# Causal attention units in three pieces of keys, with loads and context work moved

## Chip, cores and metric

One core of a Trainium2 chip runs the whole program. The metric is device time in microseconds; before is the median of three runs.

## The reference, cut to what matters

The program is a decoder of two layers over `x` of shape 4 x 512 x 256 (batch, positions, features) with a context of 4 x 1601 x 256. The change lies in the second layer's causal self-attention and its neighbours:

```python
# 4 batches, 16 heads of 16 features, T = 512
qkv = einsum('btd,ed->bte', x, w_qkv)                 # three 256-wide projections
scores = einsum('bhqd,bhkd->bhqk', q, k) * SCALE
scores = scores + (1 - tril(ones(T, T))) * -10000.0   # causal
out = einsum('bhqk,bhkd->bhqd', softmax(scores), v)
x = layernorm(x + out.reshape(b, t, 256) @ w_out.T)
# then cross-attention of the same x to 1601 context rows (rotary queries and keys, mask),
# then a layernormed feed-forward block
```

Before it come a recurrent layer, a cross-attention and a layer of eight routed experts; the change does not touch them.

## The kernel before

All of the second layer stands in `last_layer`. It is built twice, for `causal` true and false, and a flag computed on the chip chooses; the true form runs here. Its order is written out by hand (`tc.manual_schedule`): each engine executes its instructions in the order in which the code emits them.

**Units.** A unit is (batch b, group g of four heads, cross or not). `units` lists 16 self units (four batches by four groups), then 16 cross units. A group's four heads lie in four strips of 32 partitions, so that four matmuls of 32 rows can share the PE array. `qt[g]` and `kself[g]` hold queries and keys of a group; row 16 of a strip of queries holds the negated maximum of each query, so that the scores come out with the maximum subtracted.

**A self unit, before.** It has four rounds, one for each 128 keys k. A round holds, in two halves of two heads each:

- `scores(u, k, half, h)`: one matmul of keys k against the queries from k*128 on (512, 384, 256, 128 columns), line 1612, into a PSUM bank of its own;
- `next1()`: one slot of the maxima of a later unit, which are computed ahead. A slot takes two heads and one block t of 128 queries against the keys up to that block (128 to 512 columns, line 216, tile `most`), and a reduction with the causal additive mask for each head (line 1573). A self unit has eight slots; the order of t is 2, 3, 0, 1. A cross unit has 26 (line 1571);
- `exponents`: ACT's exponential per head (line 1622) and POOL's `affine_select` per half, which clears the upper triangle of the diagonal block (line 1625);
- `weighted(u, k)`, one round late: four matmuls of 32 columns each (line 1647) into one bank. ACT copies the first into `ot` (line 1657), and DVE adds the other three (line 1660).

When the last slot of a unit is done, `negated` reduces and transposes the maxima and writes them into `qt` by four small DMAs (line 1601, `nrows`). At the start of a self unit, four slots beyond its own are done (`lead`). Units 14 and 15 take one more slot per half round, so that the maxima of unit 16, the first cross unit, are ready.

All PSUM tiles of the layer come from one pool of eight banks, used in turn.

**Work between.** Four lists per unit hold other work. `starts[i]` runs at the start of unit i. `extras[i]` is spread over the rounds. `quiet[i]` gives one item per half round. What is left of either runs at the unit's end. The items that matter here:

- `self_rows(b, c)`: the projections K and Q of batch b for two groups (PE, ACT, then a write to DRAM, since heads change partitions), and `rows`, which loads keys and queries of both groups back (SP, line 1336). They lie in `extras[i+1+2c]` and `starts[i+2+2c]`, with i the first unit of batch b-1.
- `finish(u)`: `divided` (transposes of `ot` and the division); after a batch's last group also `turned`, four `projected` (projection, addition to `x`, moments), and the normalization in `quiet`; then `forward(0)` and `forward(1)` (transposes of the normalized `x`, line 1726) at the head of `extras[index[u] + 2]`.
- `combined(b)`: gathers the expert rows of batch b, adds, normalizes and transposes them.
- `context(b, keys, values)`: keys and values of the context. A key item projects (ACT line 1477), rotates (DVE shuffle and three POOL or DVE operations, lines 1443 to 1446) and writes to `kcd[b]`. A value item is a projection and ACT's copy (line 1491). Its input `cx` is loaded in chunks by ACT's queue (line 1461).
- `cross_queries(b, c)`: rotated queries for the cross units, with loads of their own.

All DMAs of SP's and ACT's queues share eight completion semaphores in turn, so a DMA also waits for the one that had its semaphore before.

**Ahead of unit 0**, the code runs the values of batch 0, some of its keys, the first `self_rows`, the self values, eight value items of batch 1. K and Q of the second pair of groups (`k1_`, `q1_`), the remaining keys of batch 0 and the loads `rows1` are at the head of `extras[0]`.

Of the kernel before, what the change touches and what calls it, by code (L numbers as in the profile page):

```python
# [17 lines left out]
P = 128  # L18
# [23 lines left out]
def decoder(ctx: ExitStack, tc: tile.TileContext, a: dict, out: bass.AP):  # L42
# [1261 lines left out]
    def last_layer(causal):  # L1304

        with ExitStack() as s4:
# [35 lines left out]
            starts = [[] for _ in range(len(units) + 3)]  # L1342
            state = {}
# [67 lines left out]
            def self_rows(b, c, tile=raw_tile):  # L1411
# [9 lines left out]
                def rows():  # L1421
                    for g in (2 * c, 2 * c + 1):
                        from_rows(kself[g], ksd[b], g)
                        from_rows(qt[g], qd[b], g)

                return [lambda: item("qkvK", ksd[b], 1.0), lambda: item("qkvQ", qd[b], QS)], rows
# [82 lines left out]
            def cross_queries(b, c):  # L1509
# [10 lines left out]
                def rows():  # L1520
                    flush(0)
                    for g in (2 * c, 2 * c + 1):
                        from_rows(qt[g], qd[b], g)

                return [item], rows


# [4 lines left out]
            def slots1(u):  # L1532
                return 2 * (1 + NT * NBIG) if u[2] else 2 * NT

            def slot1(u, s):
# [27 lines left out]
                t, c = ((i - 1) // NBIG, (i - 1) % NBIG) if cross else ((i + 2) % NT if causal else i, 0)  # L1563
                n = (t + 1) * P if causal and not cross else 512
                for j, rows, ps in tiles:
                    mm(ps[:, :n], [(qt[g][rows, t * P : (t + 1) * P], kt[rows, c * 512 : c * 512 + n])])

                def reduce():
                    for j, rows, ps in tiles:
                        if cross:  # L1570
                            nc.vector.tensor_reduce(pm[:, t, j, c : c + 1], ps, AX.X, ALU.max)  # L1571
                        else:
                            nc.vector.tensor_tensor_reduce(  # L1573
                                out=ps[:, :n],
                                in0=ps[:, :n],
# [29 lines left out]
            def scores(u, k, half, h):  # L1605
                b, g, cross = u
                kn = kn_of(k) if cross else P
                kt, q2 = keys_of(u), state["q2", u]
                ps = one("s")
                rows = slice((2 * half + h) * 32, (2 * half + h) * 32 + 32)  # L1610
                q0 = seen(u, k)
                nc.tensor.matmul(  # L1612
                    ps[:kn, q0:], kt[rows, k * P : k * P + kn], q2[rows, q0:], start=True, stop=cross or causal
                )
                return ps

            def exponents(u, k, half, pair):
                kn = kn_of(k) if u[2] else P
                ex = p4.tile([P, 2, S], F32, tag="ex", name="ex", bufs=4)
                for h, ps in enumerate(pair):  # L1620
                    q0 = seen(u, k)
                    nc.scalar.activation(ex[:kn, h, q0:], ps[:kn, q0:], AF.Exp)  # L1622
                if causal and not u[2]:
                    block = ex[:, :, k * P : (k + 1) * P]
                    nc.gpsimd.affine_select(  # L1625
                        out=block, in_=block, pattern=[[0, 2], [1, P]], compare_op=ALU.is_ge,
                        fill=0.0, base=0, channel_multiplier=-1,
                    )
                state["ex", u, k, half] = ex
# [8 lines left out]
            def weighted(u, k):  # L1638

                b, g, cross = u  # L1640
                kn = kn_of(k) if cross else P
                po = one("po")
                q0 = seen(u, k)
                for j in range(4):
                    ex = state["ex", u, k, j // 2]
                    c0 = (4 * g + j) * VW
                    nc.tensor.matmul(  # L1647
                        po[j * 32 : j * 32 + 32, q0:],
                        (vals if cross else vself)[b % 2][:kn, k, c0 : c0 + 32],
                        ex[:kn, j % 2, q0:],  # L1650
                        start=True,
                        stop=True,
                    )
# [562 lines left out]
```

## Time and profile before

| | |
|---|---|
| median of three runs | 2037.76 us (2034.16 to 2040.95) |
| the profiled execution | 2031.6 us, span 2029.7 us |
| mean granted TensorE clock | 0.989 |
| busy: PE, DVE, ACT, POOL | 1972.0, 1152.6, 1058.8, 633.7 us |
| self units (first exponent 927.1 us, first of the cross units 1215.7 us) | 288.6 us |
| cross units, first exponents | 1215.7 to 1877.0 us for the last |

How to read it: busy times are shares of one execution, and PE's ends are modelled, so that a busy PE may still wait. Durations in a group are means of one instruction. Rows of the timeline give the start, the length, the engine, the line and the tiles; a bracket gives idle time before the row and what ended it.

### The profile page before, as it was taken

How to read it: one execution, taken by the hardware profiler on the slowest of the kernel's cores; microseconds unless marked ns; L12 is line 12 of the kernel's file. 1: busy time of each engine (PE TensorE's matmuls, PEld its weight loads, DVE VectorE, ACT ScalarE, POOL GpSimd, SP SyncE). 2: the span in 40 equal slices, each digit the busy share in tenths (PEclk: the TensorE clock that was granted, in tenths of full speed). 3: DMA queues.
4: the chain of work that ended last, by engine and by line, in shares of the span. 5: the costliest groups of instructions: out<-in, count | busy, mean ns of one | idle time of the engine just before them, and what ended most of it. 6: DMA issues, size and time to landing. Idle time of an engine off the chain costs nothing.

```text
span 2029.7 us, 33782 instructions
## 1 busy us (share of the span) xinstructions
PE 1972.0 (97%) x12736; PEld 1223.4 (60%) x12736; DVE 1152.6 (57%) x2871; ACT 1058.8 (52%) x2220; POOL 633.7 (31%) x657
## 2 busy tenths in 40 slices
PE   9999999999999999988899999999999999999998
PEld 5768677787899999964455553333333433333366
DVE  3455334442233333356666697677778788887333
ACT  1111222124554555634556537787778788878631
POOL 3010001131222222234632324555655365353110
PEclk9999999999999999999999999999999999999999
DMA  9930411116887786743422111111210120102000
GB/s 365 352 105 1 165 65 54 54 68 257 308 311 292 256 323 265 291 124 109 137 59 59 51 53 42 43 47 58 76 45 28 35 87 18 33 18 85 1 11 33
DMA packets 80109, 242.61 MB, mean 120 GB/s; under 512 B 14134, under 2 KB 37084, under 8 KB 68028
## 3 DMA queue, kind: packets, MB, share of 16 engines
q1 hardware_dynamic: 59948, 141.45, 20.4%
q0 software_dynamic: 13152, 85.64, 11.1%
q10 hardware_dynamic: 6832, 13.20, 2.0%
q8 instruction: 105, 1.72, 0.3%
q14 instruction: 72, 0.59, 0.1%
HBM read 194.47 MB, written 56.69 MB: 124 GB/s over the span
## 4 chain that ended last, share of the span: by engine, by line
PE 48%; DVE 4%; ACT 1%; POOL 1%; issue 1%; DMA 1%; SPq 0%; ACTq 0%; POOLq 0%; DVEq 0%
PE one L216 12%; PE s L1612 12%; PE po L1647 11%; PE most L216 10%; DVE pm L1571 2%; DVE most L1573 1%; PE one L1678 1%; POOL x L188 1%; ACT ex L1622 1%; ACT x L178 0%; PE one L1703 0%; DVE st L163 0%; DMA kcd<-raw 0%; POOL ot L1664 0%; DVE ot L1660 0%
## 5 line engine op out<-in xcount | busy, mean ns | idle before, releaser
L1622 ACT ACTIVATE ex<-s 128x512 f32<-128x512 f32 (+4 forms) x1088 | 526.1, 565 | 177.6 <-PE most L216 97.4
L1571 DVE TENSOR_REDUCE pm<-most 128x1 f32<-128x512 f32 x768 | 477.7, 682 | 93.2 <-PE most L216 91.8
L216 PE MATMUL most<-kc,qt 32*128 32x512 f32 (+1 forms) x2048 | 425.2, 535 | 0.7 <-ACT ex L1622 0.4
L1612 PE MATMUL s<-qt,kc 32*128 32x512 f32 (+1 forms) x1664 | 409.0, 618 | 1.3 <-DMA qt<-nrows 1.3
L1664 POOL TENSOR_TENSOR ot<-ot,part 128x512 f32<-128x512 f32 x180 | 228.1, 1268 | 278.6 <-ACT part L1663 278.2
L1612 PEld LDWEIGHTS s<-qt,kc 32*128 32x128 f32 (+1 forms) x1664 | 133.8, 180 | 171.0 <-ACT ex L1622 125.4
L1647 PE MATMUL po<-ex,v 128*32 128x512 f32 (+1 forms) x1664 | 225.1, 605 | 0.0
L216 PEld LDWEIGHTS most<-kc,qt 32*128 32x128 f32 x2048 | 171.4, 185 | 53.3 <-issue 19.3
L1102 DVE TENSOR_TENSOR g<-g,sg 128x1024 f32<-128x1024 f32 (+1 forms) x38 | 45.5, 1197 | 215.3 <-ACT sg L1100 215.3
L1573 DVE CUSTOM_DVE_ANT_0 most<-most,c_diagq 128x384 f32<-128x384 f32 (+3 forms) x256 | 118.4, 519 | 39.0 <-PE most L216 28.2
L216 PE MATMUL wide<-xbT,eWg 128*128 128x128 f32 (+1 forms) x928 | 135.3, 306 | 1.9 <-ACT g L1100 1.9
L216 PE MATMUL wide<-xbT,eWi 128*128 128x128 f32 (+1 forms) x928 | 134.6, 305 | 0.0
L216 PEld LDWEIGHTS wide<-xbT,eWg 128*128 128x128 f32 x928 | 126.3, 194 | 8.7 <-ACT g L1100 2.1
L216 PE MATMUL bank<-eWo,g 128*128 128x256 f32 x592 | 130.8, 379 | 0.0
L216 PEld LDWEIGHTS wide<-xbT,eWi 128*128 128x128 f32 x928 | 125.6, 192 | 8.2 <-issue 0.8
L1647 PEld LDWEIGHTS po<-ex,v 128*32 128x32 f32 (+1 forms) x1664 | 34.5, 108 | 150.1 <-ACT ex L1622 145.3
L216 PEld LDWEIGHTS bank<-eWo,g 128*128 128x128 f32 x592 | 111.1, 190 | 14.3
L1663 ACT COPY part<-po 128x512 f32<-128x512 f32 x180 | 106.7, 593 | 7.3 <-PE po L1647 6.4
L1625 POOL TENSOR_SCALAR_AFFINE_SELECT ex<-ex 128x256 f32<-128x256 f32 x128 | 52.5, 417 | 157.2 <-ACT ex L1622 157.2
L1612 PE MATMUL s<-qt,ks 32*128 32x128 f32 (+3 forms) x512 | 97.6, 483 | 3.4 <-DVE at L1682 2.4
L709 POOL DMA_INDIRECT xs<-x,rows x32 | 31.3, 978 | 214.8 <-DVE ltot L695 153.4
L216 PE MATMUL most<-ks,qt 32*128 32x256 f32 (+3 forms) x512 | 92.6, 486 | 5.5 <-ACT v L1491 2.9
(336 smaller groups left out, 2913.9 us busy)
## 6 DMA issues: line engine op xcount, KB each, us to landing
xs<-zero SPq DMA_DIRECT2D x32, 512.0 KB
kc<-kcd SPq DMA_DIRECT2D x16, 800.5 KB
eWo<-in_eWo SPq DMA_DIRECT2D x8, 1408.0 KB
eWi<-in_eWi SPq DMA_DIRECT2D x8, 1028.0 KB
eWg<-in_eWg SPq DMA_DIRECT2D x8, 1028.0 KB
qt<-qd SPq DMA_DIRECT2D x32, 256.0 KB
ctxT<-in_ctxT SPq DMA_DIRECT2D x4, 1601.0 KB
kcd<-in_c_rowkc SPq DMA_DIRECT2D x4, 1601.0 KB
```

Source lines behind the costliest of these rows:

```text
L188: nc.gpsimd.tensor_scalar(into(t), xb[:, t, :], mid["mv"][:, t, 0:1], mid["rs"][:, t : t + 1], ALU.subtract, ALU.mult)
L216: nc.tensor.matmul(ps, l, r, start=(i == 0), stop=(i == n - 1))
L709: nc.gpsimd.indirect_dma_start(xs, bass.IndirectOffsetOnAxis(ap=rows[:, k * NT + t : k * NT + t + 1], axis=0), x[b][:, t, :], None)
L1102: nc.vector.tensor_tensor(part, part, dst, ALU.mult)
L1571: nc.vector.tensor_reduce(pm[:, t, j, c : c + 1], ps, AX.X, ALU.max)
L1573: nc.vector.tensor_tensor_reduce(out=ps[:, :n], in0=ps[:, :n], in1=diagq[:, 384 - t * P : 384 - t * P + n], scale=1.0, scalar=LOWEST, op0= ...
L1612: nc.tensor.matmul(ps[:kn, q0:], kt[rows, k * P : k * P + kn], q2[rows, q0:], start=True, stop=cross or causal)
L1622: nc.scalar.activation(ex[:kn, h, q0:], ps[:kn, q0:], AF.Exp)
L1625: nc.gpsimd.affine_select(out=block, in_=block, pattern=[[0, 2], [1, P]], compare_op=ALU.is_ge, fill=0.0, base=0, channel_multiplier=-1,)
L1647: nc.tensor.matmul(po[j * 32 : j * 32 + 32, q0:], (vals if cross else vself)[b % 2][:kn, k, c0 : c0 + 32], ex[:kn, j % 2, q0:], start=True ...
L1663: nc.scalar.copy(part, po)
L1664: nc.gpsimd.tensor_tensor(state["ot"], state["ot"], part, ALU.add)
```

## The change

A causal self unit has three pieces instead of four rounds: keys 0, keys 2, and keys 1 and 3 together. In the joint piece the scores of a head are two matmuls into one bank (keys 1 in columns 128 to 511, keys 3 in columns 0 to 127), with one exponential of 512 columns, one select over two diagonal blocks, and weighted sums that accumulate both keys in one bank. The maxima have three groups, t = 2 and 0 in one bank, 1, and 3; a unit has six slots, and units 14 and 15 take two more per half.

The loads of keys and queries are split by group: the first group's is issued at the end of the unit that makes them, the second's at the start of the next. For batch 0's cross queries, the first group's load moves one unit forward. `forward` moves one unit back. The gathers of batches 2 and 3 are split six and five between two units instead of eight and three. Ahead of unit 0 come the remaining keys of batch 0, `k1_`, `q1_` and the loads `rows1`, with two value items instead of eight; the other values and some keys of batch 1 move to the extras of units 0 to 3.

```diff
+            def pieces(u):
+                if causal and not u[2]:
+                    return [(0,), (2,), (1, 3)]
+                return [(k,) for k in range(NKT if u[2] else NT)]
+            groups = [(2, 0), (1,), (3,)] if causal else [(t,) for t in range(NT)]
+            def spans(u, ks):
+                if len(ks) == 1:
+                    return [(ks[0], seen(u, ks[0]), seen(u, ks[0]), S)]
+                return [(k, seen(u, k), 0 if i else seen(u, k), S - seen(u, k) if i else S) for i, k in enumerate(ks)]
...
-                return 2 * (1 + NT * NBIG) if u[2] else 2 * NT
+                return 2 * (1 + NT * NBIG) if u[2] else 2 * len(groups)
...
+                for t, cols, n in wide_:
+                    for j, rows, ps in tiles:
+                        mm(ps[:, cols], [(qt[g][rows, t * P : (t + 1) * P], kt[rows, :n])])
...
-                nc.tensor.matmul(
-                    ps[:kn, q0:], kt[rows, k * P : k * P + kn], q2[rows, q0:], start=True, stop=cross or causal
-                )
+                for k, q0, c0, c1 in spans(u, ks):
+                    kn = kn_of(k) if cross else P
+                    nc.tensor.matmul(
+                        ps[:kn, c0:c1], kt[rows, k * P : k * P + kn], q2[rows, q0:], start=True, stop=cross or causal
+                    )
...
+                for i, (k, q0, e0, e1) in enumerate(parts):
+                    kn = kn_of(k) if cross else P
+                    for j in range(4):
...
+                            start=i == 0,
+                            stop=i == len(parts) - 1,
...
-                    extras[index[u] + 2].insert(0, lambda: forward(0))
-                    extras[index[u] + 2].insert(1, lambda: forward(1))
+                    extras[index[u] + 3].insert(0, lambda: forward(0))
+                    extras[index[u] + 3].insert(1, lambda: forward(1))
...
-                    quiet[i - 2] += summed[:8]
-                    quiet[i - 1] += summed[8:]
+                    quiet[i - 2] += summed[:6]
+                    quiet[i - 1] += summed[6:]
...
-                    starts[i + 2 + 2 * c].append(rows)
+                    soon[i + 1 + 2 * c].append(rows[0])
+                    starts[i + 2 + 2 * c].append(rows[1])
...
-                    starts[i + 2 + 2 * c].append(rows)
+                    starts[i + (2 if b else 1) + 2 * c].append(rows[0])
+                    starts[i + 2 + 2 * c].append(rows[1])
...
-            for f in turns0 + self_values(0) + add1 + values1[:8]:
+            for f in turns0 + self_values(0) + keys0[2:4] + keys0[6:8] + [k1_, q1_]:
+                f()
+            flush(0)
+            for f in add1 + values1[:2] + rows1:
                 f()
...
-            extras[0] = [
-                k1_, q1_, *keys0[2:4], lambda: (keys0[6](), keys0[7]()), lambda: (flush(0), rows1()),
-                *values1[8:11],
-            ] + extras[0]
-            extras[1] = values1[11:] + keys1[:2] + extras[1]
-            for i, n in enumerate((2, 5)):
-                extras[i + 2] = keys1[n : n + 3] + extras[i + 2]
+            extras[0] = values1[2:9] + extras[0]
+            extras[1] = extras[1] + values1[9:] + keys1[:2]
+            extras[2] = keys1[2:5] + extras[2]
+            extras[3] = extras[3] + keys1[5:8]
+            for work, loads in zip(extras, soon):
+                work += loads
...
-                        shorter = half and causal and not u[2] and k > 1
+                        shorter = causal and not u[2] and ks == ((2,) if half else (1, 3))
...
-                        if i in (14, 15) and done["n"] < ends1[units[16]] + LEADX:
-                            reduces[half].append(next1())
+                        for _ in range(2 if causal else 1):
+                            if i in (14, 15) and done["n"] < ends1[units[16]] + LEADX:
+                                reduces[half].append(next1())
```

## The prediction

> **What bounds it now.** I read the page first, then windows cut at the first exponent of each self unit (unit 0 to 15), then groups by shape inside 926 to 1215 us, then the timeline.
>
> ```profile
> PE 1972.0 (97%) x12736; PEld 1223.4 (60%) x12736; DVE 1152.6 (57%) x2871; ACT 1058.8 (52%) x2220; POOL 633.7 (31%) x657
> ```
>
> PE is never idle for long anywhere, so 97% says little. The change touches 900 to 1216 us only: the cross units keep their instructions (the moved `forward` of the last batch is the one exception). So the question is what the 290 us of self units lose.
>
> ```profile
> core 0: us, PE busy (x) PEld busy (x) DVE busy (x) ACT busy (x) POOL busy (x), PEclk, DMA share, GB/s
> 926.00:944.43 18.43, 15.34 (x106) 8.40 (x106) 11.34 (x51) 9.69 (x27) 6.98 (x16) 0.91 0.58 184
> ...
> 966.03:990.80 24.77, 21.59 (x134) 11.24 (x128) 15.88 (x49) 10.16 (x24) 21.34 (x24) 0.93 0.54 168
> ...
> 1007.86:1027.51 19.65, 16.55 (x133) 9.74 (x127) 15.44 (x69) 12.06 (x32) 3.25 (x8) 1.00 0.25 69
> 1027.51:1043.22 15.71, 15.57 (x121) 8.64 (x121) 8.83 (x31) 9.65 (x24) 5.51 (x9) 0.89 0.08 18
> ...
> 1169.99:1215.70 45.71, 44.05 (x335) 23.59 (x336) 43.03 (x97) 14.19 (x36) 10.13 (x19) 0.96 0.16 50
> ```
>
> Second column the length, then busy time by engine. Most units are bound by no engine's sum: unit 4 (1007.86) has DVE 15.4 and PE 16.6 in 19.65, and unit 5 runs at a granted clock of 0.89. Only units 14 and 15, which also take unit 16's maxima, are DVE's (43.03 of 45.71). Unit 11 cut into its four rounds shows why a unit without accidents is long:
>
> ```profile
> 1121.72:1125.80 4.08, 4.08 (x36) 2.07 (x32) 1.50 (x9) 2.66 (x5) 0.81 (x2) 1.00 0.00 0
> ...
> 1132.63:1135.50 2.87, 2.85 (x28) 1.41 (x23) 2.87 (x9) 0.89 (x5) 0.81 (x2) 1.00 0.54 161
> ```
>
> The first round (scores 512 wide, maxima 128) is PE's, with DVE 1.5 of 4.08; the last (scores 128, maxima 512) is DVE's, 2.87 of 2.87. Eight banks do not carry work across rounds, so a unit pays the larger engine round by round.
>
> ```profile
> 1018.44 3.72 PE L216 MATMUL one<-outP,atT 128*128 128x256 f32 x16
> ...
> 1024.76 0.30 ACT L132 ACTIVATE sd<-mv,eps 128x4 f32<-128x4 f32 x1 [5.69 <-DVE mv L168]
> ...
> 1027.51 2.02 ACT L1622 ACTIVATE ex<-s 128x512 f32<-128x512 f32 x4
> 1027.65 0.98 PE L1726 MATMUL one<-ident,x 128*128 128x128 f32 x5 [0.16 <-ACT x L178]
> ```
>
> The end of unit 4 (8 and 12 alike): the projection ends at 1022.1, DVE is still at four 512-wide maxima (1018.3 to 1021.0) and reaches the moments late; ACT stands 5.69 us, and the next unit's exponents start 5.4 us after the projection. PE stands on `forward`'s transposes meanwhile, and the clock falls in the next unit.
>
> **The change, part by part.** Rounds are A (piece 0, 512 wide), B (piece 2, 256), C (1 and 3, 384+128).
>
> ```profile
> L1622 ACT ACTIVATE ex<-s 128x512 f32<-128x512 f32 x64 | 33.4, 596 | 23.2 <-PE s L1612 21.6 <-PE most L216 1.4
> ...
> L1622 ACT ACTIVATE ex<-s 128x384 f32<-128x384 f32 x64 | 27.0, 493 | 10.4 <-PE s L1612 10.3
> ...
> L1622 ACT ACTIVATE ex<-s 128x128 f32<-128x128 f32 x64 | 14.3, 275 | 26.8 <-PE s L1612 26.2 <-POOL ex L1625 0.5
> ```
>
> *Instructions removed.* 64 exponents of 384 and of 128 become 64 of 512: 64 x (493+275-596) ns = 11.0 us of ACT. One 128-wide addition a unit goes: 16 x 0.267 us (the shortest row of L1660) = 4.3 us of DVE. Selects go from eight to six a unit, two of them over 512 elements; the trace has only 256 (417 ns), so those cost 417 to 834 and POOL saves 0 to 13 us. Columns on PE and maxima on DVE stay. ACT and POOL end last nowhere in the self units, so this alone is worth 0, save DVE's 0.5 us in units 14 and 15.
>
> *One round fewer.* DVE's maxima per round become 4x512, 4x(384+128), 4x256, beside scores of 512, 256 and 512 columns: the wide maxima no longer meet the narrowest scores. In unit 11, PE's own work is four bursts of scores and maxima at 1.35 (the burst from 1117.55 to 1118.9) = 5.4, weighted sums 0.99+0.78+0.59+0.39 = 2.75 (chain of waits), two projections of 1.91 and transposes of 0.59: 12.6 of 13.78. At most 1.2 us goes; I take 0.8 for units 7 and 11: **1.6**.
>
> *Units 4, 8, 12.* The projection now meets 256-wide maxima: 4 x about 0.38 instead of 4 x 0.65 on DVE, and they precede it, so the moments follow the projection by 1.3 us, not 2.6. I take 1.3 + 0.4 for the round = 1.7 each: **5.1**. ACT's wait stays, since the applies still precede the exponents.
>
> *`forward` one unit later.* Units 5 and 9 lose 0.98 us of transposes; at clock 0.89 over 15.71 they lost 1.7 us, which may stay if the gap stays. I take 2.4 each for round, transposes and part of the clock (bounds 1.0 to 3.5) and 1.5 for unit 13 (at 0.75 now): **6.3**. Units 6 and 10 take the 1.0 over.
>
> *Requests at the end of the unit.* In the changed program's instruction order SP issues these loads in the same sequence as before (rows of nrows, K and Q writes, loads); what changes is the distance to the user. For batch 1, and the second halves of batches 2 and 3, K and Q now stand in an early round: no wait. For the first half of batches 2 and 3, Q is made in unit 5's and 9's last round and used by the maxima of round B of units 6 and 10.
>
> ```profile
> 1107.02 0.61 SPq L1333 DMA_DIRECT2D qd<-raw  x1
> ...
> 1111.57 0.33 SPq L1336 DMA_DIRECT2D qt<-qd  x1
> ```
>
> Write to load issue takes 4.5 us, and the maxima using it start at 1114.43, 8.0 us after Q's evacuation began (1106.39). The new distance is round A, `forward` and two weighted sums, about 5.5: a wait of 2.5. With the transposes taken over I charge 1.0 in unit 6 (which waits 2 already) and 2.2 in unit 10 (bounds 0 to 4 each): **-3.2**.
>
> *More keys, fewer values ahead.* The same PE work in another order. Now the key writes of two chunks pass SP inside unit 0, and ACT's load of `cx` stands behind one of them: ACT idles 4.25 us until 933.44, and PE drops to 0.91. In the new order POOL turns those keys from about 907 and SP has them out by 919, before the maxima of unit 0 end; `nrows` of unit 0 stands behind them and four loads. Those loads wait for the K and Q writes until about 922, DVE's maxima end near 923, so the first scores come 0.8 us later than 926.0 (0 to 4 if POOL is late). Unit 0 then needs about 11.5 us plus its lead against 18.43: 5.0 net. Two values slip into unit 1 (-0.9). Unit 2 loses part of its clock loss (24.77 x 0.07 = 1.7) and a round of waiting behind POOL: 3.3 (0 to 5); unit 3, 1.5. Sum **8.9**.
>
> *Units 14 and 15.* DVE's floor is 43.0-0.5 = 42.5; three slots a half round instead of two use up the slots that ran alone before unit 16: 1.7 of the 3.2 possible. **1.7**.
>
> Sum: 1.6+5.1+6.3-3.2+8.9+1.7 = 20.4, taken as 20. The profiled execution took 2031.6 us (span 2029.7), 6.2 below the median of 2037.76; against itself the change gives 2011.6, against the median **2018**.
>
> **A rule that speaks against it.** In C each head's 384 columns are followed by its own 128, and only then by the next head's 384. Both stand on one row group, so the second head must overtake waiting passes.
>
> ```profile
> 1121.48 0.37 PE L216 MATMUL most<-ks,qt 32*128 32x128 f32 x1
> 1121.59 0.59 PE L1612 MATMUL s<-qt,ks 32*128 32x512 f32 x1
> 1121.70 0.54 PE L216 MATMUL most<-ks,qt 32*128 32x128 f32 x3
> 1122.01 0.59 PE L1612 MATMUL s<-qt,ks 32*128 32x512 f32 x1
> ```
>
> Here both heads' scores stand before both maxima in the program, yet three passes of maxima start ahead of the last pass of scores. So matmuls of other row groups do overtake, one or two waiting ones at least; I take no cost. The Trainium skill (TensorE: Matmul & The Clock Gate, Part 3: Packing small matmuls) states the opposite: matmuls start in program order and only weight loads are pulled ahead. By that rule the sum would be rival 1's 2052 instead of 2018.
>
> **Rivals.**
> 1. *Slower: the joint scores run one head after another.* If three waiting passes cannot be overtaken, C loses its pairs. Passes on one row group follow at 0.54 us for 512 columns and 0.21 for 128 (1120.50 to 1121.04, 1120.83 to 1121.04), so about 0.43 for 384; a head takes 2 x (0.43+0.21) = 1.28, two in turn 2 x 1.28 - 0.21 = 2.35, so 1.07 more, twice a unit, 16 units: 34 us, and 2018+34 = 2052. It decides from about 0.6 us a half. Chance 0.12; another 0.05 for lesser losses (Q's wait at 4 us and a late start).
> 2. *Little gain.* A fills all eight banks and is followed by 2.6 us of maxima; bubbles join rather than vanish, and ACT's 5.69 us stays. Then only unit 0's 5.0 and some 2 elsewhere remain, minus 3.2: 2034. Chance 0.25, 0.16 of it faster, 0.09 the same.
> 3. *The earlier request does nothing*, since SP's order is the same; its part of the forecast is already negative, so this rival lies inside the forecast.
> 4. *More:* no half clock left and units at PE's own work: 15 us beyond, 2003. Chance 0.08.
>
> **How the numbers follow.** Forecast 0.50 (2011 to 2026). What can be told from no change is 0.3%, 6 us. Faster 0.50+0.08+0.16 = 0.74, the same 0.09, slower 0.17. The range goes from rival 4's 2003 to 2042, the milder losses; only rival 1 lies outside.
>
> **What would show it.** Exponents of 512 in round C; unit 4 near 17.9 us and unit 11 near 13; the gap of ACT before `sd` under 5 us; units 6 and 10 longer, with PE waiting for `qt<-qd`; no ACT idle before 940 due to `cx`; the second head's 384 starting within 0.2 us of the first's. It is wrong if that distance is about a microsecond, or if units 5 to 13 keep their lengths.

## The result, and the profile after

The changed kernel takes 2052.34 us in the median of five runs (2047.41 to 2055.32) against 2037.76. Compared over all runs and not by the two medians alone, it takes 1.0061 times as long, 95% interval 1.005 to 1.0072. It is slower, where a gain of 20 us was forecast. The profiled execution took 2052.93 us (span 2051.2, mean granted clock 0.980 instead of 0.989).

The page's first part: ACT lost 7 us of work (11.0 were forecast) and POOL 4, DVE gained 7, and PE counts 6 us more for the same 12736 matmuls.

```profile
PE 1978.2 (96%) x12736; PEld 1230.0 (60%) x12736; DVE 1159.6 (57%) x2855; ACT 1051.9 (51%) x2156; POOL 629.6 (31%) x625
```

Windows cut at the first exponents, with the columns of before: units 1, 4, 8, 9, 10 and 11, and then 14 with 15.

```profile
950.85:980.48 29.63, 25.98 (x145) 14.06 (x147) 10.78 (x42) 11.38 (x25) 6.20 (x10) 0.83 0.28 90
1021.65:1047.96 26.31, 20.88 (x140) 12.37 (x140) 18.27 (x75) 11.81 (x27) 5.79 (x14) 0.87 0.18 51
1093.20:1116.35 23.15, 20.03 (x141) 12.04 (x138) 16.98 (x68) 11.72 (x28) 3.35 (x7) 0.93 0.11 37
1116.35:1128.66 12.31, 11.61 (x105) 6.64 (x108) 7.86 (x32) 8.05 (x18) 2.91 (x6) 1.00 0.10 24
1128.66:1148.36 19.70, 16.91 (x128) 10.65 (x124) 9.90 (x38) 8.39 (x20) 5.19 (x7) 0.83 0.24 69
1148.36:1160.23 11.87, 11.87 (x110) 6.21 (x103) 9.82 (x38) 7.22 (x16) 2.27 (x5) 1.00 0.22 55
1189.74:1234.60 44.86, 44.60 (x331) 24.92 (x327) 42.45 (x85) 14.66 (x30) 11.95 (x17) 0.96 0.17 55
```

Units 9 and 11 run at full clock and, unit 11, at PE's own 11.87 us: there the change did what it promised. Units 4 and 8 (19.65 us in unit 4 before) and 10 are far longer, at clocks of 0.83 to 0.93 and with PE idle for 2.8 to 5.4 us.

The whole sum, in us, by the first exponent of each unit; `before_again` is a second profile of the kernel before (span 2034.9), taken with the experiments:

| part | forecast | after, less the first profile of before | less its second |
|---|---|---|---|
| up to the first `x<-x,nb,rstd` (a normalization on ACT) ahead of unit 0 | 0 | +4.4 | +1.6 |
| from there to the first exponent, units 0 to 3 | -8.9 | +6.2 +3.2 | +5.2 +1.8 |
| units 4, 8, 12 | -5.1 | +9.0 | +8.9 |
| units 5, 9, 13 | -6.3 | -10.9 | -10.9 |
| units 6, 10 | +3.2 | +10.4 | +10.6 |
| units 7, 11 | -1.6 | -2.6 | -2.6 |
| units 14, 15 | -1.7 | -0.9 | -0.9 |
| from unit 16 on | 0 | +2.6 | +2.6 |
| sum (of the unrounded parts) | -20.4 | +21.5 | +16.3 |

From 500 us on the trace of after has 75.3 us at half clock, those of before 37.9 and 48.5. Half of the difference, 13 to 19 us, is what PE can lose by that (an estimate from these lengths); the loss is 16 to 21.

The three units of the row 4, 8 and 12 differ: unit 4 grew by 6.7 us, unit 8 by 3.3, and unit 12 fell by 1.0.

**Units 4, 8, 12.** The timeline at the end of unit 8 (start, length, engine, line, tiles; in brackets idle time and what ended it):

```profile
1106.24 1.09 ACT L1738 COPY atT<-one 128x512 f32<-128x512 f32 x2
1106.89 5.46 PE L216 MATMUL one<-outP,atT 128*128 128x256 f32 x16 [1.70 <-ACT atT L1738]
1108.48 0.42 DVE L1744 TENSOR_TENSOR x<-one,x 128x256 f32<-128x256 f32 x1 [2.73 <-PE one L216]
1113.60 0.30 ACT L132 ACTIVATE sd<-mv,eps 128x4 f32<-128x4 f32 x1 [6.27 <-DVE mv L168]
1116.35 2.02 ACT L1648 ACTIVATE ex<-s 128x512 f32<-128x512 f32 x4
```

The projection `outP` stands behind the last round with nothing beside it. PE waits 1.70 us for the last transposed copy, then runs the sixteen passes in 5.46 us instead of 3.72, since 3.4 us of them are at half clock, and DVE waits for their results instead of being late with its maxima. ACT's gap before `sd` is 6.27 (5.69 before). Unit 4 has the same end, and before it one more wait, for queries, as in units 6 and 10 below:

```profile
1028.22 1.34 PE L216 MATMUL most<-ks,qt 32*128 32x384 f32 x16 [2.41 <-DMA qt<-qd]
```

In unit 12 the projection stands behind the last round too, but PE neither waits nor loses its clock there (3.78 us, ACT's gap 4.58), and the unit takes 19.95 us instead of 20.91. There the place of the projection by itself costs nothing that shows.

**Units 6, 10.** The timeline at the start of unit 10:

```profile
1127.61 0.61 SPq L1333 DMA_DIRECT2D qd<-raw  x1
1132.19 0.33 SPq L1336 DMA_DIRECT2D qt<-qd  x1
1134.89 2.11 PE L216 MATMUL most<-ks,qt 32*128 32x384 f32 x16 [2.79 <-DMA qt<-qd]
1136.73 1.09 PE L1638 MATMUL s<-qt,ks 32*128 32x256 f32 x4
1137.88 0.66 ACT L1648 ACTIVATE ex<-s 128x256 f32<-128x256 f32 x2 [5.03 <-PE s L1638]
```

Write to load takes 4.58 us (4.55 before), and the maxima want the queries 2.79 us before they are there. That is the wait that was forecast (2.5). Behind it PE runs at half clock (1134.9 to 1141.7; four score passes of 256 columns end 1.09 us after the first starts, 0.70 at full clock), and this unit's scores stand behind the waiting maxima, so ACT loses 5.03.

**Unit 1** waits for a load that held PE for 1.25 us at most before (in the second profile):

```profile
968.83 0.38 ACTq L1462 DMA_DIRECT2D cx<-in_ctxT  x1
970.23 0.38 ACT L1492 COPY v<-one 65x256 f32<-65x256 f32 x1
973.39 5.37 PE L216 MATMUL one<-cx,xaK 128*128 128x512 f32 x8 [3.65 <-DMA cx<-in_ctxT]
```

The values end the use of one `cx` and the keys at once ask for the next, which ACT's queue requests only behind ACT's exponents. Here, too, a step of half clock falls on the eight passes behind the gap: they take 5.37 us, 3.70 in unit 1 of `cx_apart` below, at full clock.

### The profile page after: what moved, and what is told of

It reads as the page before. It is cut to its first block, busy times and chain, and to the rows that moved or that the text cites. A ratio compares the mean times of both kernels' runs of the same rounds, so it can differ in the third digit from the quotient of the medians.

```text
span 2051.2 us, 33601 instructions
## 1 busy us (share of the span) xinstructions
PE 1978.2 (96%) x12736; PEld 1230.0 (60%) x12736; DVE 1159.6 (57%) x2855; ACT 1051.9 (51%) x2156; POOL 629.6 (31%) x625
## 4 chain that ended last, share of the span: by engine, by line
PE 48%; DVE 3%; POOL 2%; ACT 2%; DMA 2%; issue 1%; another core or an unknown queue 0%; SPq 0%; ACTq 0%; POOLq 0%; DVEq 0%
PE s L1638 12%; PE one L216 12%; PE po L1678 11%; PE most L216 10%; DVE pm L1584 1%; PE one L1710 1%; ACT x L178 1%; POOL x L188 1%; DMA qt<-qd 1%; ACT ex L1648 0%; DVE most L1599 0%; DMA qd<-raw 0%; POOL raw L1447 0%; POOL swp L1446 0%; POOL raw L1445 0%
## 5 line engine op out<-in xcount | busy, mean ns | idle before, releaser
L1648 ACT ACTIVATE ex<-s 128x512 f32<-128x512 f32 (+2 forms) x1024 | 519.2, 589 | 166.9 <-PE most L216 106.6
L1655 POOL TENSOR_SCALAR_AFFINE_SELECT ex<-ex 128x256 f32<-128x256 f32 (+1 forms) x96 | 46.5, 487 | 184.3 <-ACT ex L1648 184.1
L216 PE MATMUL most<-ks,qt 32*128 32x512 f32 (+3 forms) x512 | 85.5, 488 | 11.3 <-DMA qt<-qd 8.3
```

Of the source, the lines that this page charges most:

```text
L216: nc.tensor.matmul(ps, l, r, start=(i == 0), stop=(i == n - 1))
L1648: nc.scalar.activation(ex[:kn, h, c0:], ps[:kn, c0:], AF.Exp)
L1655: nc.gpsimd.affine_select(out=block, in_=block, pattern=pattern, compare_op=ALU.is_ge, fill=0.0, base=0, channel_multiplier=-1,)
```

## The experiments

Ratios are to the kernel before, run alongside on the same chip. Four chips were used, and the median of the kernel before is 2033.4 and 2034.1 us on two of them (chips 1 and 3), 2038.9 to 2039.3 on the others (5 and 6); so ratios can be compared between experiments, times cannot. A is the round of keys 0, B of keys 2, C of keys 1 and 3.

### Is the slow stretch ahead of unit 0 the change's?

`again` is the changed kernel unaltered, `before_again` the kernel before.

> The changed kernel once more, unaltered, for a second profile. In the first profile the products ahead of the first self unit stood still from 877 to 892 us (ACT's copies of v waited 14 us in all) and the first exponent came at 937.7 us, 41.5 us after the first x<-x,nb,rstd. If that standstill is chance, it is absent here, the first exponent comes at about 928 to 932, still 41.5 us (within 1) after x<-x,nb,rstd, and the time is about 2043 to 2048. If it belongs to the changed program it recurs, and the time is about 2052. In both cases units 4, 6, 8 and 10 are as long as in the first profile (26.3, 19.8, 23.1, 19.7 us, each within 1.5).

> The kernel before, unaltered, for a second profile. In its first profile the stretch from the first product of v to the first x<-x,nb,rstd took 18.0 us and began at 873.9 us; in all five profiles of the changed kernel and its variants so far it began at 865.8 to 868.5 and took 27.6 to 27.8 us, with PE standing still in the products of v. If the standstill belongs to the changed program, it is absent here, and the time is about 2032 to 2038. If the first profile of before was the exception, the stretch begins at about 866 and takes 27 us here too, the first exponent comes near 929, and the time is about 2035 to 2040.

2050.57 and 2036.78 us. From the first product of `v` to `x<-x,nb,rstd` the first profile of before had 18.0 us; its second has 26.1, the two of after 27.8 and 27.6. In the later profiles the stretch takes 17.7 to 19.2 or 25.9 to 27.8 us, and it goes with the chip: all eight profiles on chips 1 and 3 have the short length, all nine on chips 5 and 6 the long one, `before_again` among them (for the first profiles of before and after the chip is not recorded). So this is not the change's, and the second profile is the fairer comparison. Why the chips differ stays open. Units 4, 6, 8 and 10 of `again` are as long as in the first profile of after (25.5, 19.3, 23.3 and 19.5 us).

### Which part costs?

`old_ahead`: the order of the work ahead of unit 0, `extras[0]` to `extras[3]` and the split of the gathers as before.

```diff
-quiet[i - 2] += summed[:6]
-quiet[i - 1] += summed[6:]
+quiet[i - 2] += summed[:8]
+quiet[i - 1] += summed[8:]
...
-for f in turns0 + self_values(0) + keys0[2:4] + keys0[6:8] + [k1_, q1_]:
-    f()
-flush(0)
-for f in add1 + values1[:2] + rows1:
+for f in turns0 + self_values(0) + add1 + values1[:8]:
     f()
...
```

> The changed kernel with the order of work ahead of unit 0 and the keys and values in units 0 to 3 as before the change. Theory: the new order is a loss, since four more rotations of keys stand ahead of the sums of x and of unit 0's maxima: the first exponent comes 35 to 36 us after the first x<-x,nb,rstd instead of 41.5, units 0 to 3 take about 81 us in all instead of 84, and the time falls by 9 us to about 2043. Rival: the order is neutral, unit 0 grows by what the start gains (unit 0 was 17.3 us before and is 13.1 now), and the time stays at 2049 to 2053. Units 4 to 15 are as in the changed kernel in both.

1.0035 (1.0022 to 1.0048), median 2045.5: the new order costs some 5 us as it stands. From `x` to the first exponent is again 36.2, but units 0 to 3 take 91.2 instead of the 81 expected. The waits of units 0 and 1 say why:

```profile
PE most L216 <- DMA qt<-qd: 12.5, 1, 12.5
```

With three rounds unit 2's maxima begin in the second of unit 0's three rounds (the third of four before), before the queries made at the head of `extras[0]` are loaded. So with three pieces either order costs: the old one 12.5 us of waiting in unit 0, the new one the later start and unit 1's wait. The old one is the cheaper, by some 5 us.

`three_alone`: the kernel before with three pieces and nothing else (the old order as above, `forward` and all requests as before).

> The kernel before with three pieces and three groups of maxima alone; forward, requests and the order ahead of unit 0 as before. Theory: three rounds alone cost 8 to 16 us: units 0 to 3 take about 91 us in all instead of 80.7, units 4, 8 and 12 are 2 to 6 us longer each, units 5, 9 and 13 about 2 shorter; the time is 2046 to 2054. Rival: the pieces alone gain their round (2 to 6 us) and the time is 2032 to 2037.

1.0083 (1.0065 to 1.0101): 17 us slower than before, the most of all (8 to 16 were expected). Unit 0 has the same wait (10.6 us), and units 6 and 10 take 35.2 (29.1 before). `four` undoes only the pieces and the maxima's groups; the order of maxima and scores in a round and the slots of units 14 and 15 go back with them:

```diff
-return [(0,), (2,), (1, 3)]
+return [(0,), (1,), (2,), (3,)]
...
-groups = [(2, 0), (1,), (3,)] if causal else [(t,) for t in range(NT)]
+groups = [(2,), (3,), (0,), (1,)] if causal else [(t,) for t in range(NT)]
...
```

> The changed kernel with four pieces and four groups of maxima as before, and all else as changed (forward a unit later, requests at the end of the unit, more keys ahead). Theory: it is the cut to three rounds that costs, since what was spread over four rounds falls behind the last one or meets its own load: units 4, 8 and 12 come back to 18 to 20 us each, units 5, 9 and 13 stay below before's (13 to 14.5), unit 1 falls from 27 to 29 us to about 20, and the time is 2030 to 2036, below before. Rival: the other three parts cost as much as the pieces; the time is 2042 or more.

1.007 (1.0055 to 1.0086), no better, where a time below before's was expected. Units 4, 8 and 12 fall from 69.4 to 60.1, which shows that the three rounds, with their three groups of maxima, are what costs there; units 5, 9 and 13 rise from 34.2 to 42.8. The two nearly cancel. `four_old` is `four` with the old order ahead as well, so that only the later `forward` and the earlier requests remain of the change:

> Four pieces and the order ahead of unit 0 and in units 0 to 3 as before the change; forward a unit later and the requests at the end of the unit as changed. Theory: with four rounds these two parts gain at most their transposes in units 5, 9 and 13 (2 to 3 us in all) and lose 2 to 7 us in units 6 and 10: the time is 2037 to 2044, so the 13 us that the run with four pieces lost came mostly from the order ahead of unit 0. Rival: they lose as much as the order ahead, 2044 or more; or they gain 6 us and more, 2033 or less.

1.005 (1.0033 to 1.0066). This was the rival's side: with four rounds the two remaining parts cost some 10 us, in units 0 to 3 (86.6) and 6 (22.05). In unit 6 of `four`, which has the later `forward` too, POOL's bias addition lies on DVE's weighted additions of the gathers:

```profile
1062.05 2.37 POOL L1763 TENSOR_TENSOR x<-x,bob 128x1024 f32<-128x1024 f32 x1
1062.35 3.60 DVE L1386 SCALAR_TENSOR_TENSOR x<-y,ws,x 128x256 f32<-128x256 f32 x2
...
1067.03 0.70 PE L1638 MATMUL s<-qt,ks 32*128 32x256 f32 x4 [2.98 <-DVE at L1714]
```

The first of the two additions takes 3.06 us there; without an instruction on POOL one takes 0.48. DVE reaches its other work later, and PE waits 2.98 us for DVE's division (3.13 in `four_old`).

`forward_back` and `requests_back` each undo one of these in the changed kernel:

```diff
# forward_back
-extras[index[u] + 3].insert(0, lambda: forward(0))
+extras[index[u] + 2].insert(0, lambda: forward(0))
...
# requests_back
-soon[i + 1 + 2 * c].append(rows[0])
-starts[i + 2 + 2 * c].append(rows[1])
+starts[i + 2 + 2 * c] += rows
...
-starts[i + (2 if b else 1) + 2 * c].append(rows[0])
+starts[i + 2 + 2 * c].append(rows[0])
```

> The changed kernel with forward where it was, two units after the last of its batch. Theory: inside three rounds the later forward is a gain, as it was forecast (6.3 us, less 2 us that units 6 and 10 take over): units 5, 9 and 13 grow from 12.3, 12.3 and 9.6 to about 14.3, 14.3 and 10.4 us, units 6 and 10 fall by about 1, and the time rises by 3 to 6 us to 1.0075 to 1.009 of before's. Rival: the part costs, as with four pieces, because x<-x,bob on POOL now meets the sums of x on DVE in unit 6: the time falls by 3 us or more, to 1.0045 or less.

> The changed kernel with all requests for queries and keys at the start of the next unit. On SP the self units' sequence stays the same; on PE the division of units 5 and 9 moves back to the third round, and nothing else of the self units moves. Theory: the request by itself does nothing: units 4 to 13 keep their lengths within 1 us, the time stays within 3 us of the changed kernel's (1.0046 to 1.0076 of before's). Rival: as items of the list the requests shift the work beside them, and without them the time falls by 4 us or more.

1.0037 (1.0024 to 1.0049) and 1.0053 (1.0035 to 1.0071). `forward` at its old place is 0.24% better than the change, and 0.16% better than `requests_back`, which ran on the same chip; the second difference lies within the two intervals. Units 5, 9 and 13 pay 2.6 us together, but units 6 and 10 take 32.0 instead of 39.5. There the transposes are gone, and the wait for the queries, though it stays (2.10 and 1.93 us), leaves one step of half clock in unit 6 instead of two, and none in unit 10:

```profile
1127.84 1.17 PE L216 MATMUL most<-ks,qt 32*128 32x384 f32 x16 [1.93 <-DMA qt<-qd]
```

The same sixteen passes took 2.11 us behind 2.79 of waiting. The earlier requests make no difference that can be told.

### The three waits, taken away one by one

`weighted_first`: in units 4, 8 and 12 the items of round A run behind its weighted sums, so that `finish`'s pauses fall one round earlier.

```diff
+early = i in (4, 8, 12) and k == 0
-if k and u[2]:
+if k and u[2] or early:
     weighted(*due)
...
-if due and not (k and u[2]):
+if due and not (k and u[2] or early):
     weighted(*due)
```

> The changed kernel, with the last weighted sum of units 3, 7 and 11 issued ahead of the items of the first round of units 4, 8 and 12, so that division, transposes and projection of a batch take one round each of the three. Theory: in the changed kernel the two pauses need four rounds, so the projection falls behind the last round and runs alone (1106.2 to 1112.3 us in unit 8, at half clock, while DVE and ACT mostly wait). Units 4, 8 and 12 fall from 26.3, 23.1 and 20.0 us to 18 to 20 each, 10 to 14 us in all, and the time to about 2040. Rival: ACT's wait for the moments and the clock set these units, not the place of the projection: they fall by under 1.5 us each and the time to no less than 2047.

1.0015 (1.0003 to 1.0026), 2041.52: by the ratio 9.4 us off the change, as expected. Unit 4:

```profile
1018.76:1041.32 22.56, 19.25 (x140) 11.99 (x140) 18.32 (x75) 11.82 (x27) 5.76 (x14) 0.92 0.19 61
...
1033.28 3.72 PE L216 MATMUL one<-outP,atT 128*128 128x256 f32 x16
...
1038.57 0.30 ACT L132 ACTIVATE sd<-mv,eps 128x4 f32<-128x4 f32 x1 [2.55 <-DVE mv L168]
```

The projection lies beside round C at full clock, and ACT's gap falls from 6 us to 2.55. The three units take 63.4 us (22.6, 21.4 and 19.5) instead of 69.4: 6.0 less, where 10 to 14 were expected; units 6 and 10 fall as well, by 3.4 together. In unit 4 the wait for the queries is gone too, and PE waits 2.22 us for DVE instead, so this run does not separate the projection's place from the waits.

`q_early`: Q's projection of units 5 and 9 directly behind K's, in round B, so that its write has a round more.

```diff
-into.insert(min(1, len(into)), divided)
+into.insert(min(2 if index[u] in (4, 8) else 1, len(into)), divided)
```

> The changed kernel, with Q of units 5 and 9 right behind K in the second round and the division in the third. SP's order is unchanged. Theory: the write of Q leaves about 4.5 us earlier, so PE's wait for qt<-qd in units 6 and 10 (2.8 us each) is gone, and with it the half clock of 6.8 us that follows each: units 6 and 10 fall from 19.8 and 19.7 us to 13.5 to 15.5, and the time by 9 to 12 us to about 2041. Rival: the wait and the half clock have separate causes: only the 2.8 us go, units 6 and 10 come to about 17 and the time to about 2047.

1.0001 (0.9991 to 1.0012), 2039.51: by the ratio 12 us off the change. Unit 10:

```profile
1125.51:1139.41 13.90, 13.90 (x131) 8.84 (x127) 10.07 (x38) 8.42 (x19) 5.31 (x8) 1.00 0.22 75
```

19.70 us become 13.90: no idle PE, full clock. The wait itself was 2.79. Unit 6, for which the same was expected, only falls from 19.8 to 18.5: its wait for the queries and its half clock are gone as well, but PE now waits up to 1.5 us at a time for DVE and its own issue. So the two units give 7 of the 12 us in this profile, and where the rest lies is not shown.

`lead2` reaches the same from the other side: the maxima lead the scores by two half groups instead of four.

```diff
-return LEADX if u[2] else 4
+return LEADX if u[2] else 2
```

> The changed kernel with two half groups of maxima computed ahead of a self unit instead of four. Theory: four half groups were two of four rounds and are two of three now, so the maxima of the unit after next ask for its queries and keys a third of a unit earlier than before; with two the wait for qt<-qd in units 4, 6, 8 and 10 is gone (2.4 to 2.9 us each) and the half clock behind it: units 6 and 10 fall from 19.5 to 14 to 16 us, and the time by 6 to 12 us to 2040 to 2046. Rival: the row of maxima (nrows) now reaches its unit's scores too late, and each of 15 units waits 0.5 to 2 us for qt<-nrows: the time stays at 2048 or rises to 2070.

1.0021 (1.0007 to 1.0034), 2039.13; PE waits for no `qt<-qd` in the self units any more, and unit 10 takes 13.5 us. Unit 6 takes 18.7, more than the 14 to 16 expected: the gathers' additions lie beside POOL's bias addition there, as in `four` (the first takes 3.56 us, and PE waits 2.65 for DVE). Units 4, 8 and 12 take 63.0 us (23.3, 20.0 and 19.6), as little as with `weighted_first`, though the projection stays behind round C. A lead of four half groups was two of four rounds and is two of three now: the same number asks for the queries earlier. Units 5, 9 and 13 pay 2.6 us for the shorter lead.

`fix2` is `weighted_first` with `q_early`.

> The changed kernel with both repairs, the weighted sum first in units 4, 8 and 12, and Q right behind K in units 5 and 9. If the two losses are separate they add: each took 9 to 12 us off the changed kernel's time, so 2027 to 2033, below before. If they share their half clocks (units 6 and 10 were already shorter with the first repair alone), the sum is 2033 to 2039.

0.9988 (0.9975 to 1.0001): the two add in part, to the time before (the second of the two cases).

`cx_apart` puts unit 1's own work between the last value and the first key:

```diff
-extras[0] = values1[2:9] + extras[0]
-extras[1] = extras[1] + values1[9:] + keys1[:2]
+extras[0] = values1[2:11] + extras[0]
+extras[1] = values1[11:] + extras[1] + keys1[:2]
```

> The changed kernel with two more values in unit 0 and the last two first in unit 1, so that the first key of batch 1 comes a round or more after the item that asks for its cx. Theory: the wait for cx (4.4 us) and the half clock behind it (two of three windows of 3.4 us there) go: unit 1 falls from 27.3 to 19 to 21 us, unit 0 grows by 1 to 3, and the time falls by 4 to 6 us to 1.003 to 1.0045 of before's. Rival: POOL, busy for 25 of unit 2's 27 us with the turns of the keys, takes it over: unit 2 grows by what unit 1 loses, and the time stays at 1.0052 or more.

1.0012 (1.0 to 1.0024), 2035.72: by the ratio 10 us off the change, more than expected. Unit 1 falls from 29.6 us (27.3 in `again`) to 19.2 at full clock; unit 0, which takes over two value items, grows by 0.5 to 13.7. The wait itself was 3.65. Unit 1's window:

```profile
944.86:964.05 19.19, 19.19 (x139) 10.52 (x140) 11.23 (x42) 10.55 (x23) 5.31 (x9) 1.00 0.37 109
```

### The later start

`sums_first` runs the sums `add1` ahead of the remaining keys, as before:

```diff
-for f in turns0 + self_values(0) + keys0[2:4] + keys0[6:8] + [k1_, q1_]:
+for f in turns0 + self_values(0) + add1 + keys0[2:4] + keys0[6:8] + [k1_, q1_]:
```

> The changed kernel with one group moved on DVE: the eight sums of x of batch 1 (x<-ex,ws,x) stand ahead of the shuffles of the four keys that POOL turns, as before the change, not behind them. In the changed kernel they run from 918.8 to 924.3 us beside POOL's rotations (5.5 us for eight, of 3.8 without) and unit 0's maxima wait behind them on DVE, while PE had the first of them at 919.4. Theory: this order is the loss of the start; the first exponent comes 36 to 38 us after the first x<-x,nb,rstd instead of 41.4, units 0 to 3 keep their 84 to 85 us, and the time falls 3 to 5 us to about 2047. Rival: the maxima wait for the queries and keys or for PE anyway: the start moves by under 1.5 us, the time stays at 2050 to 2053.

1.0049 (1.0033 to 1.0066). From `x` to the first exponent 40.2 instead of 41.4, not the 36 hoped for. SP's queue took the place of the sums: unit 0's last maxima end at 923.94 already, but its `nrows` stand on SP behind the four loads of `rows1`, which wait for the K and Q writes.

```profile
923.21 0.73 DVE L1599 CUSTOM_DVE_ANT_0 most<-most,c_diagq 128x512 f32<-128x512 f32 x1
...
925.18 0.42 SPq L1336 DMA_DIRECT2D qt<-qd  x1
...
925.73 2.31 SPq L1627 DMA_DIRECT2D qt<-nrows  x4
...
930.75 1.22 PE L1638 MATMUL s<-qt,ks 32*128 32x512 f32 x2 [3.29 <-DMA qt<-nrows]
```

`fix3` adds `sums_first` to `fix2`:

> The changed kernel with three repairs: the weighted sum first in units 4, 8 and 12, Q right behind K in units 5 and 9, the sums of x ahead of the shuffles. If the start's loss adds to the others: 2031 to 2035, below before. If the start is hidden behind other waits in units 0 to 3: 2035 to 2038.

0.9991 (0.9975 to 1.0008), no different from `fix2`. The start's 5 us stay with this order.

### A version that beats both

`best` is the change with `lead2`, `weighted_first`, `sums_first` and `cx_apart`; `best_forward_back` has `forward` at its old place besides.

> The changed kernel with four repairs: two half groups of maxima ahead instead of four, the weighted sum first in units 4, 8 and 12, the sums of x ahead of the shuffles, the first key of batch 1 apart from its cx. If the losses add: 0.991 to 0.995 of before's time. If the half clocks come back at other places: 0.996 to 1.000.

> The kernel with the four repairs, and forward back at two units after the last of its batch. If the later forward costs by itself, as in the changed kernel (its time fell by 0.24% without it), the ratio falls from 0.9974 to 0.995 to 0.996. If it cost only through the wait for qt<-qd and the half clock in units 6 and 10, which the repairs have taken away, it is a gain here, as forecast: units 5, 9 and 13 grow by 0.9 each, the ratio is 0.998 to 0.9995.

`best`: 2027.6 us, 0.9974 of the kernel before (0.9957 to 0.9991; 2034.1 us on that chip); the change is at 1.0061, so these four edits are worth about 0.9%. That is the case in which half clocks come back elsewhere. PE waits for no `cx` and no `qt<-qd` in its self units any more. `best_forward_back`: 1.0 (0.9989 to 1.0011), on another chip. With the four repairs the later `forward` is thus ahead by 0.26%, though undoing it in the change as given brought 0.24%. The intervals of each pair all but touch, so the turn is likely and not certain. By the units the gain is not where it was forecast: without the later `forward` units 5, 9 and 13 take 3.3 us more and units 6 and 10 3.4 less (in unit 6 the gathers' additions no longer meet POOL's bias addition, and the unit takes 14.2 instead of 16.7), and the rest of the difference is half clock, in units 4, 8 and 15 and behind unit 16 above all (85.0 us of it from 500 us on against 39.7).

## Why the prediction was wrong

Two terms of the sum that were booked as gains came out as losses, the start with units 0 to 3 and units 4, 8 and 12, and a third, units 6 and 10, was priced far too low. Against the second profile of before they are 16, 14 and 7 us off. The last two, and the wait in unit 4, come from one wrong step: the prediction did not follow the distances that are written as a number of rounds or slots (a pause in a chain, the lead of the maxima) through a unit of three rounds; and it priced a wait of PE at its length, without the half clock behind it.

- **Units 4, 8, 12: the failed step.** The prediction had the projection beside the 256-wide maxima and took 1.7 off each unit. No maxima lie beside it at all. `finish` runs at the end of A, its division and first pause end in B, its transposes and second pause in C, and the projection falls behind C; four rounds had room for two pauses and the projection, three have not. In unit 8 PE then waits 1.70 us for the transposed copy and meets the half clock. In unit 4 it also waits 2.41 us for queries, though the prediction says "no wait" for batch 1. +9.0 instead of -5.1, in units 4 and 8 alone (+6.7, +3.3, and -1.0 in unit 12). That three rounds cost this is shown by `four`, which takes all of it back. How it divides is not: `weighted_first`, which moves the projection, takes 6.0 back, and `lead2`, which leaves it and moves the maxima, 6.4.
- **Units 6, 10: the right wait, the wrong price.** A wait of 2.5 us was forecast and 2.79 came in unit 10, but the charges of 1.0 and 2.2 became 4.4 and 6.1. What was left out is what the wait does to the clock and to the scores queued behind the waiting maxima. The bound of "0 to 4 each" was too tight: without the wait, unit 10 is 5.8 us shorter.
- **Start and units 0 to 3.** Unit 0 gained 4.2 us on the first profile of before and 5.7 on the second (13.1 us), where 5.0 was forecast. The start came 5 to 6 later, not 0.8. Counted from the first `x<-x,nb,rstd`, the forecast had unit 0's maxima done after 31 us and the loads `rows1` after 30. It put POOL's keys and SP's loads in the sum but not DVE's `add1` sums, which moved behind the keys (they start after 22.5 us instead of 12.1) and of which eight take 5.48 us instead of 3.75 beside POOL's rotations: the maxima end after 36. And SP's loads were put too early: the last is issued after 33. In `sums_first` the maxima are done after 31, as forecast, but the loads still end after 32.5, and only 1.2 us come back; so both terms were too small, and the loads alone hold the start back nearly as long. The prediction also looked for `cx` in unit 0, where it is gone, and not in unit 1, where the same load now waits: +8.0 (5.8 in `again`) where +0.9 was charged. Unit 2's gain of 3.3 did not come (25.1 and, in `again`, 27.4 against 24.8).
- **Units 5, 9, 13 and 7, 11** were right in mechanism and undersized. In units 5, 9 and 13 before has 13.7 us at half clock and after none, so some 6.8 of the 10.9 us gained are the clock's, of which the forecast took only a part. By the runs the three rounds are worth 8.6 us there (`four` has 42.8) and the later `forward` 2.6 (`forward_back` has 36.8).
- **Rival 1 did not come**, and that its 2052 is the measured median is chance. The joint scores of both heads start 13 ns apart:

```profile
1123.38 0.60 PE L1638 MATMUL s<-qt,ks 32*128 32x384 f32 x2
...
1124.54 0.27 PE L1638 MATMUL s<-qt,ks 32*128 32x128 f32 x1
```

  The passes of the two heads run side by side; the next pair of passes starts 0.43 us later (1123.80). So waiting matmuls were overtaken, against the rule that the prediction quotes. The slower side came by another way: none of the rivals held that a pause or a load's distance is counted in rounds.
- **Rival 2** (little gain) had the bubbles and ACT's gap right (5.69 us before, 6.27 in units 4 and 8), but not that new waits come with three rounds.
- **Rival 3** (the earlier request does nothing) held: `requests_back` is not to be told from the change.
- **From unit 16 on** 2.6 us were not forecast; the profile of after has one stretch of 6.8 us at half clock near 1821 us there.

Left open: why the stretch of `v` ahead of unit 0 has two lengths on different chips, how the loss of units 4 and 8 divides between the projection's place and the waits, and whether another order on SP would give the start's 5 us back. No run tried that, nor the shorter lead (`lead2`) together with the old order ahead of unit 0.

## What to carry to other kernels

Before rounds are merged, count the rounds that each chain with pauses needs, and look at every distance that is written as a number of slots: with fewer rounds a chain has fewer places for its pauses, and a lead of the same number of slots asks for its input earlier in the unit before. In these runs a new wait of PE that was long enough for the clock to fall cost about twice its length (2.79 us of waiting, 5.8 us in unit 10) or more, so it is worth taking away before anything else is judged: the later `forward` cost 0.24% beside the waits and was 0.26% ahead without them, each only just clear of the noise.

## What the runs showed of the hardware

- **The clock falls for less than an idle window.** Half-clock stretches in these traces begin on a grid of 3.413 us and last one or more of its steps. Counted over the traces of these runs from 500 to 2000 us: after a window of the grid (one step) at full clock in which PE was busy for under 40%, the next was at half clock in 80 of 80 cases; between 40 and 55% in 35 of 58; between 55 and 95% in 61 of 492; above 95% in 10 of 7417. So a wait of some 2 us, 60% of a window, can cost nearly as much again: a window at half clock loses half its work, 1.7 us. Unit 10 had two windows at half clock, 3.4 us lost, behind its 2.79 of waiting, which together are near the 5.8 that `q_early` gains there. The Trainium skill (TensorE: Matmul & The Clock Gate, Part 1: The HAM clock gate) states the free-running window of 3413 ns and the half rate, as here, but puts the fall after at least one idle window. Here 18 of the 80 windows were idle, while in 53 PE was busy for 5% or more, in the one ahead of unit 10's half clock for 18%.
- **DVE slows beside POOL.** The weighted additions of 128x256 from 880 us on take 0.475 to 0.487 us in all 146 cases, over all traces, in which no instruction on POOL overlaps them. Beside POOL's tensor operations they take up to 3.06 us in unit 6 of `four` and 3.75 in unit 6 of `four_old`, both beside the bias addition of 2.37 us (their longest in after is 1.47, in before 2.22).
